# A conditional residual stack on one core: norm weights placed later, weight and output loads moved to the GpSimd queue, a third keys buffer and a fourth early product

## The chip, the cores and the metric

The program runs on one core of a Trainium2 chip. The time is the device time of one execution in microseconds (us). A core has a matrix engine (TensorE, PE in the rows; PEld is its weight load), VectorE (DVE), ScalarE (ACT), GpSimd (POOL) and SyncE (SP). SP issues most of the transfers, GpSimd issues the gathers. All data is float32.

## What is computed

`x` is 64 sequences of 32 rows by 512. Four layers follow one another, each added to its input:

```python
x = x + einsum('bct,bcd->bdt', x, L0_weights[condition])            # a 32x32 mix of the rows per sequence
x = x + x @ base.T + bias + (x @ A[adapter].T) @ B[adapter].T       # a linear layer with a low-rank part
# attention: 32 query heads, 8 key heads, D = 128, 512 cached keys by page table, 32 new ones
q, k, v = x @ Wq.T, x @ Wk.T, x @ Wv.T
q, k = rope(rmsnorm(q, q_norm_w), pos), rope(rmsnorm(k, k_norm_w), pos)
scores = where(valid, q @ concat(k_cache[table], k).T / sqrt(D), -1e30)
x = x + (softmax(scores) @ concat(v_cache[table], v)) @ Wo.T
x = x + einsum('bct,bcd->bdt', x, L3_weights[condition])            # the mix of rows again
```

## The kernel before

The 2048 rows are 16 tiles `t` of 128 rows, four sequences each. The key heads are in two groups `g` of four. A *step* is a tile of one group, 32 in all; a *unit* is one sequence of a step, 128 in all; a *slot* is one key head of a unit, 512 in all (n = 512). Slots before 0 hold the first layers, and after the last slot comes the output stage.

The order on each engine is written by hand. `at(slot, where, do, ...)` puts a piece of work into a plan, and `slot(i)` (L1120) emits the pieces of slot i in a fixed order: fetch, pool, then the scores of slot i, the transposes of slot i - 2, the projections (`pe`), powers, value products of slot i - 3, softmax division, VectorE work (`dve`), ScalarE work (`act`), stores (`store`). Each engine runs its own instructions in that order and waits where an operand is not there.

**First layers.** `First` (L380) makes one tile: the gather `mix_rows`, the block diagonal `mix_diag` of it on VectorE (L402), the matmul `mix_ps` (L411), the gathers `a_rows` and `b_rows`, transposes (L428), the low-rank product `h_ps` and the linear product `l_ps` with `base_sb` (L465). Beside them `angles()` (L296) loads the norm weights (`q_raw`, `k_raw`) and makes from them `q_cos`, `q_sin`, `k_cos`, `k_sin`, then the sines and cosines of all positions; it is a generator, taken on by `next(more)` between the slots (L1185 to L1190). In the prologue (L1153) the base weights (1 MB) and the bias are loaded ahead of it.

**Steps.** A pair of steps is projected together (`Plain` L559, `Block` L626) in the slots before it is used; the last projections are in slot 478. `Norm` scales and rotates the heads; its `rstd` (L683) is computed on GpSimd. `Unit` (L742) loads the 16 key pages of a sequence (`kT`, 64 KB each, L763) on SP into one of two buffers, at slot 4(u - 1); GpSimd gathers four blocks of values (`v_sb`, L105) in slots 4u - 1 to 4u + 2, into eight buffers. `store` (L897) writes the outputs `oT` of a step (1 MB) once in 16 slots.

**Weights.** They lie in spaces tagged w0 to w8, each reused: w6, w7 and w8 hold the angles first, then sums of query weights (`block_sum`). In the last pair of each group the next weights (`wv`, `wk`, `wq`, and at the end eight `wo`) are loaded in halves of 512 KB on SP, at fixed places after the pair's home slot (L1016).

**Output stage.** It multiplies 2 x 2 blocks with seven products instead of eight (L1281): a11, a12, a21, a22 are the outputs of two tiles and two groups (`o_in`, 1 MB each, loaded in halves by `fetch_o` while slots still run), s3 and two further sums are made of them (L1308 to L1312), and `third_weights` makes one weight combination. A product is 16 steps of 128x128 by 256 columns. Three of these products (`p1` of pairs 1, 2 and 0) are taken early, in slots 488 to 511 (`early_product`, L1090); pair 0's second product is the first of the output stage (L1317).

Of the kernel before, what the change touches and what calls it, by code (L numbers as in the profile page):

```python
# [27 lines left out]
F32 = mybir.dt.float32  # L28
# [23 lines left out]
NG = 2  # L52
# [25 lines left out]
def resid_kernel(  # L78
# [102 lines left out]
    def load_kv_weights(g, kind, i):  # L181

        if i == 0:
            w_sb[kind] = wpool.tile(
                [P, NC, KG * D], F32, name=f"w{'kv'[kind]}{g}", tag=f"w{kind}"
            )
        nc.sync.dma_start(
            out=w_sb[kind][:, :, i * 2 * D : (i + 1) * 2 * D],
            in_=wkv[2 * g + i][:, :, kind * 2 * D : (kind + 1) * 2 * D],
        )  # L190

    def load_q_weights(g, k, i):
        if i == 0:
            w_sb["q", k] = wpool.tile([P, NC, REP * D], F32, name=f"wq{g}_{k}", tag=f"w{2 + k}")
        part = slice(i * NC // 2, (i + 1) * NC // 2)
        nc.sync.dma_start(out=w_sb["q", k][:, part], in_=wq[KG * g + k][:, part])

    def load_o_weights(k, i):
        if i == 0:
            tag = f"w{(1, 0, 2, 3, 4, 5, 6, 7)[k]}"  # L200
            w_sb["o", k] = wpool.tile([P, REP, HID], F32, name=f"wo{k}", tag=tag)
        part = slice(i * REP // 2, (i + 1) * REP // 2)
        nc.sync.dma_start(out=w_sb["o", k][:, part], in_=wo[k][:, part])
# [21 lines left out]
    with ExitStack() as l2:  # L225
# [70 lines left out]
        def angles():  # L296
# [3 lines left out]
            for name, src, scale in (("q", q_norm, -SCALE * ROOT), ("k", k_norm, ROOT)):  # L300
                raw = start_pool.tile([P, 2, D // 2], F32, name=f"{name}_raw")
                nc.sync.dma_start(out=raw.rearrange("p a b -> p (a b)"), in_=across(src, D))
                for what in ("cos", "sin"):
                    norm_w[name, what] = start_pool.tile(
                        [P, 2, D // 2], F32, name=f"{name}_{what}"
                    )
                swapped = norm_w[name, "sin"]
                nc.vector.tensor_scalar(norm_w[name, "cos"], raw, scale, None, ALU.mult)
                nc.vector.tensor_scalar(swapped[:, 0, :], raw[:, 1, :], -scale, None, ALU.mult)
                nc.vector.tensor_scalar(swapped[:, 1, :], raw[:, 0, :], scale, None, ALU.mult)  # L310
            freq = start_pool.tile([P, D // 2], F32, name="freq")
            nc.sync.dma_start(out=freq, in_=across(inv_freq, D // 2))
            pos = start_pool.tile([P, NT], F32, name="pos")
# [11 lines left out]
            yield  # L325
# [33 lines left out]
            sine(0)  # L359

# [150 lines left out]
        last_scores = []  # L511

# [229 lines left out]
        class Unit:  # L742


            def __init__(self, u):
# [6 lines left out]
                self.kT = room["kT"].tile([P, NPP + 1, KG, PSIZE], F32, name="kT")  # L752
# [224 lines left out]
        for i in range(n_pairs):  # L977
# [31 lines left out]
            if p == NT // 2 - 1:  # L1009

                if g == NG - 1:
                    loads = [(load_o_weights, k) for k in range(2 * KG)]
                else:
                    loads = [(load_kv_weights, g + 1, k) for k in (1, 0)]
                    loads += [(load_q_weights, g + 1, k) for k in range(KG)]
                for w, load in zip((6, 11, 21, 23, 32, 34, 36, 38), loads):  # L1016
                    for j in (0, 1):
                        at(home + w + j, "store", *load, j)
# [37 lines left out]
        for c in range(NT):  # L1056

            home = -27 + c
            key = -1 - c
            at(home - 3 if c > 3 else begin + 2, "fetch", make, turn_of, key, Turn, 0, c, start_pool, (4, 2))  # L1060
            at(home, "turn", call, turn_of, key, "turn")
            at(home, "keep", call, turn_of, key, "keep")
            at(home + 1, "store", call, turn_of, key, "store")
            at(begin + 11 + c // 2, "dve", rotary, c)
            at(begin + 11 + c // 2, "store", store_rotary, c)
        for u in range(len(units)):
            at(KG * (u - 1) if u else ready, "fetch", make, unit_of, u, Unit, u)
# [11 lines left out]
        def fetch_o(name, g, t, i):  # L1079
            if i == 0:  # L1080
                early[name] = o_pools[0].tile([P, KG * REP, P], F32, name="o_in", tag=name)
            part = slice(i * KG * REP // 2, (i + 1) * KG * REP // 2)
            nc.sync.dma_start(out=early[name][:, part], in_=o_dram[g][t][:, part])
# [6 lines left out]
        def early_product(pair, name, i):  # L1090
            if i == 0:
                early["p1", pair] = ps_m.tile([P, HID], F32, name="proj_ps", tag="m")
            nc.tensor.matmul(  # L1093
                early["p1", pair][:, : HID // 2],
                lhsT=early[name][:, i, :],
                rhs=w_sb["o", i // REP][:, i % REP, : HID // 2],
# [4 lines left out]
        def early_keep(pair):  # L1101
            ps = early["p1", pair]
            early["p1", pair] = o_pools[0].tile([P, HID // 2], F32, name=f"p1_{pair}")
            nc.scalar.copy(early["p1", pair], ps[:, : HID // 2])  # L1104

        home = n - 24
        for j, (pair, name) in enumerate(((1, "a12"), (2, "a21"), (0, "a11"))):
            for i in (0, 1):
                at(home - 3 + 3 * j + i, "store", fetch_o, name, 0, 2 * pair, i)
            for i in range(KG * REP):  # L1110
                at(home + 8 * j + i // 2, "pe", early_product, pair, name, i)
            at(home + 8 * j + 7, "act", early_keep, pair)
        for i in (0, 1):
            at(home + 9 + i, "store", fetch_o, "a12", 1, 0, i)
            at(home + 12 + i, "store", fetch_o, "a22", 1, 1, i)
            at(home + 17 + i, "store", fetch_o, "a21", 0, 1, i)
# [36 lines left out]
        with tc.manual_schedule(engines=ENGINES):  # L1153
# [12 lines left out]
            slot(begin)  # L1166
            lora["base"] = first_pool.tile([P, NC, HID], F32, name="base_sb")
# [3 lines left out]

            lora["mask"] = []
            for i in (0, 1):

                mask_i = first_pool.tile([P, P], I32, name=f"mask_i{i}")
                nc.gpsimd.iota(
                    mask_i, pattern=[[-RANK, NB], [0, S]], base=-i * P // 2, channel_multiplier=1
                )
                low = small.tile([P, P], F32, name="mask_low", bufs=1)
                mask = first_pool.tile([P, P], F32, name=f"lora_mask{i}")  # L1180
                nc.vector.tensor_scalar(low, mask_i, 0.0, None, ALU.is_ge)
                nc.vector.tensor_scalar(mask, mask_i, float(RANK), None, ALU.is_lt)
                nc.vector.tensor_tensor(mask, mask, low, ALU.mult)
                lora["mask"].append(mask)
            more = angles()  # L1185
            next(more)
            for i in range(begin + 1, begin + 11):
                slot(i)
                for _ in range(2 if i < begin + 6 else 1):
                    next(more, None)  # L1190
# [43 lines left out]
    with ExitStack() as l3:  # L1234
# [46 lines left out]
        with tc.manual_schedule(engines=ENGINES):  # L1281
            waiting = []
            for pair in range(NT // 2):
# [33 lines left out]
                p_2 = product(a12, w21)  # L1317
# [110 lines left out]
```

## Time and profile before

| | us |
|---|---|
| median of 3 runs | 2552.29 (2546.11 to 2552.34) |
| the profiled execution | 2539.27 |
| its span | 2537.5 |

By stage, TensorE's busy time in windows of the span:

| window, us | what runs | PE busy, us | DVE busy, us | granted clock | GB/s |
|---|---|---|---|---|---|
| 0 to 63.4 | first layers begin | 42.76 | 36.56 | 1.00 | 276 |
| 63.4 to 126.8 | first layers | 59.51 | 40.53 | 1.00 | 275 |
| 126.8 to 200 | first layers end | 67.09 | 41.52 | 1.00 | 198 |
| 500 to 1000 | steps, group 0 | 499.65 | 365.20 | 1.00 | 195 |
| 1060 to 1085 | change of group | 22.58 | 17.48 | 1.00 | 255 |
| 1500 to 2000 | steps, group 1 | 499.32 | 368.33 | 1.00 | 186 |
| 2000 to 2050 | last projections, wo loads | 41.77 | 35.15 | 0.95 | 238 |
| 2050 to 2100 | last steps | 45.74 | 23.58 | 0.91 | 239 |
| 2100 to 2150 | last steps | 40.66 | 30.26 | 0.93 | 152 |
| 2200 to 2537.5 | output stage | 333.54 | 107.85 | 1.00 | 98 |

A row of the timeline has start, duration, engine (SPq is SP's queue of issues), line, operation, written and read tiles, form, count, and in brackets the idle time before it with what ended it. A busy TensorE is not one at its peak, since its matmuls are pipelined.

### The profile page before, as it was taken

The numbers are of one execution on the slowest core, as the hardware profiler recorded it, in microseconds if no ns is written. First come the engines' busy times: TensorE is split into PE (matmuls) and PEld (weight loads), VectorE is DVE, ScalarE is ACT, GpSimd is POOL, SyncE is SP. The second block draws the span as 40 slices with busy tenths as digits, with TensorE's granted clock in tenths as the row PEclk, the third lists the DMA queues.
The fourth block names the chain that finished last, engine by engine and source line by source line (L and its number), as shares of the span: only waits on it lengthen the run. The fifth ranks groups of instructions, "written<-read, shape, count | busy, mean of one in ns | idle before, by whom it ended". The sixth has DMA issues, their size and how long they took to land.

```text
span 2537.5 us, 46802 instructions
## 1 busy us (share of the span) xinstructions
PE 2473.9 (97%) x13824; PEld 1869.8 (74%) x13824; DVE 1665.4 (66%) x4150; ACT 1280.2 (50%) x3669; POOL 1072.5 (42%) x880
## 2 busy tenths in 40 slices
PE   6999999999999999999999999999999988999999
PEld 3556777777777777777777777777777777888887
DVE  5656767676767677777777677777776845533322
ACT  1336666666666666666666666666666643000000
POOL 4325555454545445454545545545554532000000
PEclk9999999999999999999999999999999989999999
DMA  8866666666667667766565556566666775333221
GB/s 276 275 193 200 189 192 187 190 194 186 200 189 205 177 199 215 255 185 201 165 192 169 181 174 186 168 183 180 182 177 210 210 254 168 126 105 127 103 84 59
DMA packets 444732, 463.60 MB, mean 183 GB/s; under 512 B 50624, under 2 KB 366912, under 8 KB 436672
## 3 DMA queue, kind: packets, MB, share of 16 engines
q1 hardware_dynamic: 401216, 321.64, 40.9%
q0 software_dynamic: 43264, 138.97, 18.5%
q8 instruction: 112, 1.84, 0.3%
q14 instruction: 140, 1.15, 0.1%
HBM read 389.12 MB, written 79.69 MB: 185 GB/s over the span
## 4 chain that ended last, share of the span: by engine, by line
PE 87%; DVE 3%; DMA 2%; ACT 1%; SPq 1%; issue 1%; ACTq 0%; DVEq 0%
PE o_ps L862 17%; PE out_ps L1256 14%; PE proj_ps L626 14%; PE s_ps L807 10%; PE proj_ps L559 8%; PE s_ps L810 8%; PE pT_ps L849 8%; PE head_ps L725 3%; PE o_ps L874 2%; DMA o<-oT 1%; PE l_ps L465 1%; DVE sm L815 1%; DVE rot_a L717 1%; PE proj_ps L1093 1%; PE mix_ps L1274 1%
## 5 line engine op out<-in xcount | busy, mean ns | idle before, releaser
L105 POOL DMA_INDIRECT v_sb<-v,v_rows x512 | 523.3, 1022 | 494.3 <-PE o_ps L862 397.3
L815 DVE CUSTOM_DVE_ANT_0 sm<-s_ps,pen 128x544 f32<-128x544 f32 x512 | 370.7, 724 | 472.2 <-PE s_ps L810 466.9
L862 PEld LDWEIGHTS o_ps<-pT,v_sb 128*128 128x128 f32 x4096 | 520.7, 192 | 137.3 <-issue 134.5
L826 ACT ACTIVATE sm<-sm,top 128x544 f32<-128x544 f32 x512 | 382.5, 747 | 472.2 <-DVE top L815 471.9
L862 PE MATMUL o_ps<-pT,v_sb 128*128 128x128 f32 x4096 | 542.3, 275 | 0.6 <-DMA v_sb<-v,v_rows 0.4
L832 ACT ACTIVATE sm<-sm,share 128x512 f32<-128x512 f32 x512 | 369.9, 723 | 185.8 <-DVE share L831 183.1
L683 POOL TENSOR_TENSOR rstd<-ss,minus_half 128x4 f32<-128x4 f32 x160 | 193.7, 1210 | 473.5 <-DVE ss L681 472.2
L807 PE MATMUL s_ps<-kT,qT 128*128 128x288 f32 x1024 | 347.4, 421 | 10.3 <-DMA kT<-kT 10.1
L851 DVE COPY pT<-pT_ps 128x512 f32<-128x512 f32 x512 | 351.2, 686 | 0.8 <-PE pT_ps L849 0.8
L849 PE MATMUL pT_ps<-ident,sm 128*128 128x128 f32 x2048 | 308.2, 273 | 1.9 <-ACT p L1104 1.7
L810 PE MATMUL s_ps<-kT,qT 128*128 128x256 f32 x1024 | 305.8, 380 | 2.7 <-DMA kT<-kT 2.6
L849 PEld LDWEIGHTS pT_ps<-ident,sm 128*128 128x128 f32 x2048 | 256.6, 141 | 54.0 <-ACT sm L832 1.8
L778 POOL TENSOR_SCALAR pen<-key_f,seq_f 128x544 f32<-128x544 f32 x128 | 280.3, 2190 | 12.2 <-DMA xS<-x 1.6
L810 PEld LDWEIGHTS s_ps<-kT,qT 128*128 128x128 f32 x1024 | 194.7, 190 | 57.5 <-DMA kT<-kT 4.2
L676 ACT ACTIVATE sq<-raw 128x128 f32<-128x128 f32 x640 | 189.8, 298 | 33.6 <-DVE raw L638 29.7
L105 POOL DMA_INDIRECT mix_rows<-in_w,cond_rows x32 | 32.7, 1022 | 347.7 <-DVE mix_diag L168 301.0
L807 PEld LDWEIGHTS s_ps<-kT,qT 128*128 128x128 f32 x1024 | 155.0, 191 | 27.7 <-issue 10.9
L1307 ACT COPY p<-out_ps 128x256 f32<-128x256 f32 x5 | 1.9, 373 | 333.8 <-PE out_ps L1256 333.8
L1256 PE MATMUL out_ps<-w,o_in 128*128 128x256 f32 x768 | 167.1, 379 | 0.0
L833 DVE TENSOR_SCALAR p_new<-sm,share 128x32 f32<-128x32 f32 x512 | 148.6, 290 | 18.2
L1256 PEld LDWEIGHTS out_ps<-w,o_in 128*128 128x128 f32 x768 | 145.9, 190 | 19.8
L638 DVE TENSOR_TENSOR raw<-proj_ps,raw 128x512 f32<-128x512 f32 x224 | 150.4, 683 | 14.2 <-PE proj_ps L626 14.2
(149 smaller groups left out, 3422.4 us busy)
## 6 DMA issues: line engine op xcount, KB each, us to landing
kT<-kT SPq DMA_DIRECT2D x2048, 64.0 KB
o<-oT SPq DMA_DIRECT2D x32, 1024.0 KB
o_in<-o SPq DMA_DIRECT2D x28, 1024.0 KB
rot<-rot SPq DMA_DIRECT2D x48, 256.0 KB
page_rows<-in_kv_cache SPq DMA_DIRECT2D x32, 256.0 KB
wq<-in_wq SPq DMA_DIRECT2D x16, 512.0 KB
vn<-v_rows SPq DMA_DIRECT2D x32, 256.0 KB
v<-in_kv_cache SPq DMA_DIRECT2D x32, 256.0 KB
```

The lines of the kernel that those rows point to most:

```text
L105: nc.gpsimd.indirect_dma_start(out=dst, out_offset=None, in_=table, in_offset=bass.IndirectOffsetOnAxis(ap=index, axis=0),)
L626: nc.tensor.matmul(self.ps, lhsT=self.pair.x[x][:, half][:, c, :], rhs=blocks(self.b)[w][:, c, :], start=(c == 0), stop=(c == 1),)
L778: nc.gpsimd.tensor_scalar(self.pen, key_f, seq_f[:, self.b : self.b + 1], BIG, ALU.is_ge, ALU.mult)
L807: nc.tensor.matmul(ps[:, first:HID], lhsT=q, rhs=self.kT[:, :n1, k, :], start=True, stop=True)
L810: nc.tensor.matmul(ps[:, HID : first + LA], lhsT=q, rhs=self.kT[:, n1:, k, :], start=True, stop=True)
L815: nc.vector.tensor_tensor_reduce(out=sm, in0=ps[:, first : first + LA], in1=self.pen, scale=1.0, scalar=3e38, op0=ALU.add, op1=ALU.min, ac ...
L826: nc.scalar.activation(sm, sm, AF.Exp, bias=top, scale=-1.0, accum_out=total)
L832: nc.scalar.activation(sm[:, :L], sm[:, :L], AF.Copy, scale=share)
L849: nc.tensor.transpose(ps[:, c, :], self.sm[k][:, c * P : (c + 1) * P], ident)
L851: nc.vector.tensor_copy(pT, ps)
L862: nc.tensor.matmul(self.o_ps[k], lhsT=self.v[c][:, k * D : (k + 1) * D], rhs=self.pT[k][:, c, :], start=(c == 0), stop=False,)
L1256: nc.tensor.matmul(ps[:, :HALF], lhsT=o[:, i, :], rhs=w[i // REP][:, i % REP, :], start=(i == 0), stop=(i == KG * REP - 1),)
```

## The change

1. `angles()` issues its three small loads ahead of base and bias, and makes the norm weights last, behind the second sine. The two masks (now `own_ranks(i)`) are made in slot begin + 2, after the first diagonals; the other pieces of the angles are taken two a slot from begin + 3 on.
2. The loads of the second group's weights and of `wo`, and all of `fetch_o`, are issued by GpSimd. The last `wo` comes four slots later.
3. Units 122 and 125 put their keys into the space w8, and the keys of units 122 to 127 are fetched eight slots ahead of use.
4. Four products are taken early: `p1` of pairs 1, 2, 0 from slots 479, 488, 496, and pair 0's second product (`p2`) over slots 504 to 514. The first takes its outputs from the space w7.

```diff
-    def load_kv_weights(g, kind, i):
+    def load_kv_weights(g, kind, i, queue=nc.sync):
...
-        nc.sync.dma_start(
+        queue.dma_start(
...
-            for name, src, scale in (("q", q_norm, -SCALE * ROOT), ("k", k_norm, ROOT)):
-                raw = start_pool.tile([P, 2, D // 2], F32, name=f"{name}_raw")
-                nc.sync.dma_start(out=raw.rearrange("p a b -> p (a b)"), in_=across(src, D))
...
+            raw_of = {}
+            for name, src in (("q", q_norm), ("k", k_norm)):
+                raw_of[name] = start_pool.tile([P, 2, D // 2], F32, name=f"{name}_raw")
+                nc.sync.dma_start(
+                    out=raw_of[name].rearrange("p a b -> p (a b)"), in_=across(src, D)
+                )
             freq = start_pool.tile([P, D // 2], F32, name="freq")
             nc.sync.dma_start(out=freq, in_=across(inv_freq, D // 2))
+            yield
...
             sine(0)
+            yield
+            for name, scale in (("q", -SCALE * ROOT), ("k", ROOT)):
+                raw = raw_of[name]
...
+                nc.vector.tensor_scalar(norm_w[name, "cos"], raw, scale, None, ALU.mult)
+                nc.vector.tensor_scalar(swapped[:, 0, :], raw[:, 1, :], -scale, None, ALU.mult)
+                nc.vector.tensor_scalar(swapped[:, 1, :], raw[:, 0, :], scale, None, ALU.mult)
...
+        def own_ranks(i):
+            mask_i = first_pool.tile([P, P], I32, name=f"mask_i{i}")
+            nc.gpsimd.iota(
+                mask_i, pattern=[[-RANK, NB], [0, S]], base=-i * P // 2, channel_multiplier=1
+            )
...
+            nc.vector.tensor_tensor(mask, mask, low, ALU.mult)
+            return mask
...
-                self.kT = room["kT"].tile([P, NPP + 1, KG, PSIZE], F32, name="kT")
+                pool, tag = (wpool, "w8") if self.u in spare else (room["kT"], "kT")
+                self.kT = pool.tile([P, NPP + 1, KG, PSIZE], F32, name="kT", tag=tag)
...
-                for w, load in zip((6, 11, 21, 23, 32, 34, 36, 38), loads):
+                places = [6, 11, 21, 23, 32, 34, 36, 38]
+                if g == NG - 1:
+                    places[-1] += 4
+                for w, load in zip(places, loads):
                     for j in (0, 1):
-                        at(home + w + j, "store", *load, j)
+                        at(home + w + j, "store", *load, j, nc.gpsimd)
...
+        spare = range(len(units) - 6, len(units), 3)
         for u in range(len(units)):
-            at(KG * (u - 1) if u else ready, "fetch", make, unit_of, u, Unit, u)
+            early_by = u >= spare[0]
+            at(KG * (u - 1 - early_by) if u else ready, "fetch", make, unit_of, u, Unit, u)
...
             if i == 0:
-                early[name] = o_pools[0].tile([P, KG * REP, P], F32, name="o_in", tag=name)
+                pool, tag = (o_pools[0], name) if name else (wpool, "w7")
+                early[name] = pool.tile([P, KG * REP, P], F32, name="o_in", tag=tag)
             part = slice(i * KG * REP // 2, (i + 1) * KG * REP // 2)
-            nc.sync.dma_start(out=early[name][:, part], in_=o_dram[g][t][:, part])
+            nc.gpsimd.dma_start(out=early[name][:, part], in_=o_dram[g][t][:, part])
...
+        home = n - 33
+        for key, name, g, fetches, begins, over in (
+            (("p1", 1), None, 0, -5, 0, 8),
+            (("p1", 2), "a21", 0, 6, 9, 8),
+            (("p1", 0), "a11", 0, 9, 17, 8),
+            (("p2", 0), "a12", 1, 13, 25, 11),
+        ):
+            for i in (0, 1):
+                at(home + fetches + i, "store", fetch_o, name, g, 2 * key[1], i)
+            for i in range(KG * REP):
+                at(home + begins + i * over // (KG * REP), "pe", early_product, key, name, i)
+            at(home + begins + over - 1, "act", early_keep, key)
+        for i in (0, 1):
+            at(home + 18 + i, "store", fetch_o, "a22", 1, 1, i)
+            at(home + 20 + i, "store", fetch_o, "a21", 0, 1, i)
         home = n - 24
-        for j, (pair, name) in enumerate(((1, "a12"), (2, "a21"), (0, "a11"))):
...
             slot(begin)
+            more = angles()
+            next(more)
             lora["base"] = first_pool.tile([P, NC, HID], F32, name="base_sb")
...
             for i in range(begin + 1, begin + 11):
                 slot(i)
-                for _ in range(2 if i < begin + 6 else 1):
+                if i == begin + 2:
+                    lora["mask"] = [own_ranks(0), own_ranks(1)]
+                for _ in range(2 if i > begin + 2 else 0):
                     next(more, None)
...
-                p_2 = product(a12, w21)
+                p_2 = early.get(("p2", pair))
+                if p_2 is None:
+                    p_2 = product(a12, w21)
```

## The prediction

> **What bounds the kernel now.** I read the page's engine shares first, then TensorE's waits, the windows around those waits, the chain and the SP queue there. The page:
>
> ```profile
> PE 2473.9 (97%) x13824; PEld 1869.8 (74%) x13824; DVE 1665.4 (66%) x4150; ACT 1280.2 (50%) x3669; POOL 1072.5 (42%) x880
> ```
>
> The span is 2537.5 us, so TensorE idles for 63.6 us: that, and matmuls run at a lowered clock, is all a change without fewer matmuls can win. Its waits (us, times, longest):
>
> ```profile
> PE mix_ps L411 <- DVE mix_diag L402: 19.3, 2, 18.3
> PE s_ps L807 <- DMA kT<-kT: 10.1, 3, 4.8
> ...
> PE proj_ps L1093 <- DMA o_in<-o: 4.3, 1, 4.3
> ```
>
> One wait of 18.3 us is the start, the others are the last steps. The start, in the timeline (start, us, instruction, idle before it):
>
> ```profile
> 14.39 0.23 DVE L308 TENSOR_SCALAR q_cos<-q_raw 128x128 f32<-128x128 f32 x1 [3.75 <-DMA q_raw<-in_q_norm]
> ...
> 17.98 0.28 DVE L402 TENSOR_TENSOR mix_diag<-mix_rows,same 128x128 f32<-128x128 f32 x1
> 18.32 0.50 PEld L411 LDWEIGHTS mix_ps<-x_sb,mix_diag 128*128 128x128 f32 x2 [18.32 <-DVE mix_diag L402]
> ```
>
> VectorE takes the first diagonal only after the norm weights, and these wait for a load that stands behind 1 MB of base weights on SP. The last steps, by windows of 10 us (length, busy us of PE, PEld, DVE, ACT, POOL, clock, DMA share, GB/s):
>
> ```profile
> 2030.00:2040.00 10.00, 8.82 (x71) 7.80 (x69) 8.04 (x21) 6.48 (x14) 4.65 (x4) 1.00 1.00 379
> 2040.00:2050.00 10.00, 4.92 (x28) 3.31 (x21) 2.39 (x7) 3.16 (x8) 5.34 (x5) 0.77 0.89 240
> 2050.00:2060.00 10.00, 5.74 (x23) 4.58 (x22) 1.83 (x5) 1.56 (x3) 0.00 (x0) 0.55 0.86 280
> ...
> 2110.00:2120.00 10.00, 5.59 (x19) 4.52 (x20) 1.83 (x5) 1.56 (x3) 3.15 (x3) 0.68 0.79 245
> ```
>
> TensorE is starved twice, and its granted clock falls with it. What SP issued before the first of the two:
>
> ```profile
> 2025.79 1.45 SPq L203 DMA_DIRECT2D wo<-in_wo  x3
> ...
> 2029.84 0.33 SPq L897 DMA_DIRECT2D o<-oT  x1
> 2030.96 15.65 SPq L763 DMA_DIRECT2D kT<-kT  x16
> 2046.66 0.90 SPq L203 DMA_DIRECT2D wo<-in_wo  x2
> 2047.67 0.36 SPq L1083 DMA_DIRECT2D o_in<-o  x1
> ```
>
> Sixteen key loads need 15.65 us to issue where 9.37 us do with nothing large ahead (at 2003.11). As built, each queue's DMAs share eight completion counters in turn, so an issue waits for the transfer eight before it. SP's waits from 1990 us on agree: L763 waited 6.2 us for wo, 5.8 for o_in, 4.8 for o<-oT. The same happens once in mid-kernel: 2.4 us at 1078 us, behind wq and a store of o.
>
> **The change, part by part**, against the profiled execution (2539.27 us, of which 2537.5 is the span).
>
> *Start.* The six norm-weight operations (1.2 us) move behind the angles, the masks behind the first diagonal, the three small loads ahead of base and bias. The first diagonal now waits for its gather alone: issued at 5.04; gathers of this form land in 2.2 to 7.4 us, so at 7.2 to 12.4; by their median in the first 60 us, 5.2, I take 10. The transpose of a_rows is next in TensorE's order; that gather, issued at 6.46, lands by its median of 7.0 at about 13. Before, it started at 20.18. So the chain starts about 7 us sooner. The base weights are issued some 2 us later but are first used 4 us after the transpose. Is 7 us kept? From 40 to 200 us TensorE idles only 10 us and the DMA share is 0.6 in 40 to 50 us, so transfers catch up. VectorE is the risk: 9.6 of 10 us busy in 20 to 30 us; the same work now has less room. I take **-6.5**; ends -9 and -2.
>
> *Keys.* Units 122 and 125 use the w8 space, free after slot 478, and from 122 on keys are fetched eight slots ahead, not four. The stalls stand at slots 488 and 504, where units 122 and 126 begin; both loads followed an o store. Stall one: 5.08 + 4.26 = 9.3 us idle, plus slow matmuls (L807 took 1.30 us for 0.65, L810 1.22 for 0.59, and so on to the o_ps group 1.79 for 1.06): 3.5 us. Stall two: 1.1 + 4.4 = 5.5 idle plus 2.8 slow. Together **-21.1** if all is gone. Late next is unit 121, still fetched four slots ahead, beside wo.
>
> *Early products.* No matmul is added: one product more goes into the slots, and one leaves the end. A slot there is (chain: start, us, what):
>
> ```profile
> 2061.57 0.89 PE o_ps L862 x8
> 2062.47 0.49 PE s_ps L807 x2
> 2062.95 0.43 PE s_ps L810 x2
> 2063.38 0.44 PE pT_ps L849 x4
> ```
>
> 2.25 us, with 0.54 more in four slots, so 2.4; a product's share adds 0.87, eight times 6.95 us. Slots 479 to 487 ran from 2014.55 to about 2042.5, 28 us for nine slots of 2.4 (plus four head transposes of 0.44): VectorE set their pace. The p1 product put there uses idle TensorE time; in 2010 to 2040 that is 3.15 us, of which I take **-2.5**. Slots 504 to 514 get the 16 steps of a product over eleven slots. Their VectorE load is no smaller but earlier: s3 and the two sums of the outputs (3 x 2.29) move from slots 508 to 511 to 503 and 504, where 1.9 us of VectorE work a slot leaves 1.35; so some 4 us of stall move there, in place of the 3.8 us idle in 2130 to 2150. **-0.5**. They wait for a21, issued three slots (10 us) ahead; the half load of o_in at 2047.67 took 7.9 us to land.
>
> *Loads through GpSimd.* Forty loads of 512 KB leave SP: 12 at the change of head group, 16 of wo, 12 of o. SP's keys then wait for keys and o stores only; in mid-kernel **-2** of that 2.4. On GpSimd each costs about what a gather does: L105, 1.02 us. The Trainium skill, "SBUF — State Buffer", the 'DVE blocks DMA' trap, speaks against this: DMAs issued from GpSimd need it to write descriptors, VectorE's two-port copies lock it out, and one of 620 ns took 3100. Row: in 20 to 30 us, with VectorE 9.6 busy, gathers took at most 1.76. By the rule each load adds some 3 us to GpSimd, by the row 1.0 to 1.8. Behind it in order stand the value gathers and rstd. The tightest gather seen, issued at 2012.59, was needed at 2017.9 and stalled TensorE 0.36 us; landing is 3.8 in the median, so 1.5 us is spare. The fourth gather of a unit is the critical one. In mid-kernel three loads stand right ahead of one (slots 197, 213, 225), two more one gather further (212, 224). In the last steps there is no rstd, and the fourth gather goes out 10.5 us before use (2071.08 for 2081.6). By the row: 3 x (1.0 issue + 1.5 for 512 KB at 350 GB/s - 1.5 spare) = **+3**. By the rule 3 us of issue in place of 1.0: 9, and 15 with the two others. I take the row, which is of this kernel. Below nothing it cannot go. The loads' own waits for space cost nothing: wo7 waits for the p1 product in its space, over three slots before, a21 for the product that ends at slot 495, four before; the gathers behind them would be the ones delayed.
>
> *Bandwidth.* The Trainium skill's "DMA: Bandwidth & Descriptors", section Issuing engines are not separate DMA queues, says that all queues end on the same 16 engines, so another issuer only saves issue time. By that, bytes set the tail: about 10.6 MB passed from 2016 to 2055.6, 268 GB/s, where eight slots of 3.25 give 26 us; at an unchanged rate stall one stays, worth 12.8. The row of 2030 to 2040 shows 379 GB/s, so 28 us: 2 us short. Stall windows of 240 and 280 say that issue, not the engines, held it back. I take the row with 1 us for unit 121: **+3**.
>
> Sum: -6.5 - 21.1 - 2.5 - 0.5 - 2 + 3 + 3 = -26.6. The profiled time 2539.3 becomes 2512.7. The median shown, 2552.29, lies 13.0 above that execution; I carry this offset: **2525.7**, say 2526.
>
> **The rivals.**
> 1. *Bytes bind.* The tail stays at about 270 GB/s, stall one returns (+12.8 less the 3 counted). For it: shares of 0.86 to 0.89 within the stall, and 10 MB of loads, 2 MB of keys and values a unit, in slots 474 to 503. Against: 379 GB/s just before. 2526 + 10 = 2536; with the start's worst end as well 2540.
> 2. *Gathers starve* (slower). Values queue behind 512 KB loads on GpSimd's one queue. If a load holds a gather by the 7.9 us that o_in took, each of the five in mid-kernel stalls 7.9 + 1.0 - 1.5 = 7.4, and the lowered clock adds 3.5/9.3 of that, as in stall one: 10.2 each, 51 in all. 2526 - 3 + 51 = 2574. It decides from (26.6 + 3) / 5 = 5.9 us a load, clock included; below that the change still gains. For it: one gather already came late. Against: a lone load waits behind no other large one here.
> 3. *The start gives nothing*: VectorE or loads take back all 6.5: 2532. For it: VectorE at 9.6; against: the load it waited for goes.
> 4. *All is absorbed*: no stall at 121 or 503, start at -9: 2526 - 6 - 4 - 2.5 = 2513.
>
> **How the numbers follow.** Forecast 0.58, rival 1 0.22, rival 2 0.08, rival 3 0.06, rival 4 0.06. The range 2512 to 2545 takes in all but rival 2 and outer tails. 0.3%, about what a measurement can tell, is 7.7 us: faster is below 2544.6. Forecast, 3 and 4 give 0.69 of that, rival 1 0.17: 0.86. Rival 1's far end leaves 0.05 and rival 2's mild form 0.01 within: 0.06. Slower 0.08.
>
> **What would show it.** First mix near 10 us, first aT transpose near 13; no wait of L807 or its successor for kT at slots 488 and 504, clock 1.00 through the last steps except at slot 503; SP's sixteen key issues back near 9 to 10 us; GpSimd loads near 1 us each, and TensorE's waits for v_sb below 5 us in all. Rival 1 shows as kT or o_in waits at DMA shares near 1.0; rival 2 as o_ps waits for v_sb after a wv, wk or wq load. I am wrong if the wait moves to s3 (VectorE on a21), or if the start merely waits for other loads by 200 us.

## The result, and the profile after

| | before | after |
|---|---|---|
| median of 6 runs | 2552.17 (2546.11 to 2552.81) | 2533.80 (2529.47 to 2537.50) |
| the profiled execution | 2539.27 | 2537.50 |
| its span | 2537.5 | 2535.7 |

The ratio is 0.9932, 95% interval [0.9919, 0.9945]: 18.4 us less between the medians. The forecast was 2526, 7.8 us too low and inside its range. The two profiled executions differ by only 1.8 us, so the first question is how far they can be compared; the experiments begin there.

TensorE's waits in the kernel after (us, times, longest):

```profile
PE mix_ps L417 <- DVE mix_diag L408: 15.0, 1, 15.0
PE o_ps L883 <- ACT oT L912: 7.6, 1, 7.6
...
PE out_ps L1278 <- DVE o_in L1342: 3.2, 1, 3.2
PE proj_ps L1122 <- ACT p L1133: 3.1, 2, 2.6
...
PE o_ps L883 <- DMA kT<-kT: 1.9, 1, 1.9
```

The waits of the scores for keys, 12.7 us before, are gone, and so is the 4.3 us for `o_in`. New is a wait of 7.6 us of the value product for `oT`, the outputs of a step, which ScalarE copies out of PSUM. The start waits 15.0 us instead of 18.3, where 10 were foreseen. The last row is a value product of the last projections, at 1993 us; at the same place after_again, a second execution of this kernel, names `v_sb`. What SP issued ahead of the new wait, from the timeline of its queue (start, duration):

```profile
2022.28 25.42 SPq L784 DMA_DIRECT2D kT<-kT  x32
2047.75 0.57 SPq L806 DMA_DIRECT2D v_new<-vn  x1
2048.43 0.38 SPq L918 DMA_DIRECT2D o<-oT  x1
2049.63 17.76 SPq L784 DMA_DIRECT2D kT<-kT  x16
```

And ScalarE, in the timeline of the same kernel:

```profile
2049.22 0.36 ACT L1133 COPY p<-proj_ps 128x256 f32<-128x256 f32 x1
2057.61 0.27 ACT L909 COPY oT<-o_ps 128x128 f32<-128x128 f32 x1 [8.02 <-DMA o<-oT]
```

Units 121 and 122 are both fetched at slot 480, one four slots ahead and one eight. Their 32 key loads stand in one row on SP's queue, and behind them the store of the third-last step's `oT`, due at slot 483. `oT` has a single buffer: ScalarE may not write the next step's outputs until that store has landed, 9.2 us after it was issued. TensorE waits for ScalarE, and its clock falls, as the windows show (length, busy us of PE, PEld, DVE, ACT, POOL, clock, DMA share, GB/s):

```profile
2040.00:2050.00 10.00, 10.00 (x71) 8.86 (x70) 6.30 (x18) 5.77 (x13) 4.91 (x6) 1.00 0.87 283
2050.00:2060.00 10.00, 2.40 (x14) 2.09 (x13) 1.83 (x5) 2.10 (x5) 7.06 (x8) 0.77 1.01 378
2060.00:2070.00 10.00, 10.00 (x58) 8.66 (x58) 4.82 (x13) 3.89 (x8) 0.00 (x0) 0.89 0.66 228
```

The keys arrive in time now, but a store has taken their place as the thing that comes late. The start, in VectorE's timeline of the kernel after:

```profile
4.69 0.17 DVE L151 TENSOR_SCALAR lora_rows<-lora_rows_f 128x8 int32<-128x8 f32 x1
14.69 0.29 DVE L408 TENSOR_TENSOR mix_diag<-mix_rows,same 128x128 f32<-128x128 f32 x1 [9.83 <-DMA mix_rows<-in_w,cond_rows]
```

As foreseen, the first diagonal waits for its gather alone. But that gather, issued at 5.02, takes 9.7 us until VectorE starts, not the 5 of the forecast.

### The profile page after: what moved, and what is told of

Read it like the earlier page. It is cut to its first block, busy times and chain, and to the rows that moved or that the text cites. A ratio compares the mean times of both kernels' runs of the same rounds, so it can differ in the third digit from the quotient of the medians.

```text
span 2535.7 us, 46802 instructions
## 1 busy us (share of the span) xinstructions
PE 2479.9 (98%) x13824; PEld 1873.1 (74%) x13824; DVE 1664.8 (66%) x4150; ACT 1279.8 (50%) x3670; POOL 1096.5 (43%) x920
## 4 chain that ended last, share of the span: by engine, by line
PE 89%; DMA 2%; DVE 2%; ACT 1%; issue 1%; POOL 0%; SPq 0%; DVEq 0%; ACTq 0%
PE o_ps L883 17%; PE proj_ps L646 15%; PE out_ps L1278 14%; PE s_ps L828 10%; PE pT_ps L870 8%; PE s_ps L831 8%; PE proj_ps L579 8%; PE head_ps L745 3%; PE o_ps L895 2%; PE l_ps L471 1%; DMA kT<-kT 1%; PE proj_ps L1122 1%; DMA v_sb<-v,v_rows 1%; PE s_ps L863 1%; PE mix_ps L1296 1%
## 5 line engine op out<-in xcount | busy, mean ns | idle before, releaser
L799 POOL TENSOR_SCALAR pen<-key_f,seq_f 128x544 f32<-128x544 f32 x128 | 281.0, 2196 | 12.7 <-DMA xS<-x 1.4
```

The costliest lines, as they stand in the source:

```text
L799: nc.gpsimd.tensor_scalar(self.pen, key_f, seq_f[:, self.b : self.b + 1], BIG, ALU.is_ge, ALU.mult)
```

## The experiments

### Are the two executions comparable?

The kernels before and after were each run once more.

> The kernel before, profiled a second time. The first profiled execution took 2539.3 us, some 13 us less than the median of the other executions (2552.2), while that of the kernel after (2537.5) stands 4 us above its median. Theory A: the execution shown was lucky, and a second one, near 2550 us, has the missing time as longer idles of TensorE at the waits for keys (slots 488 and 504, about 2040 to 2125 us). Theory B (a rival): the missing time is spread over the whole kernel as short waits or slower matmuls, so the windows up to 2010 us are longer by most of 10 us and those behind it are as they were. Theory C: it is again near 2539 us and the two offsets differ by what lies outside the span.

Measured: 2537.88, on a chip where 43 runs of before have the median 2541.0. None of the theories saw the cause: the time depends on the chip, or on the occasion, since each chip was used on one. Before has medians of 2541.0, 2550.0 and 2540.3 us on the three chips of the experiments, and had 2552.2 in the first comparison. Its profiled execution of 2539.3 fits the two quick chips, so the 13.0 us that the forecast carried as an offset are most likely a distance between chips.

> The kernel after once more, beside before on the same chip. Chips differ: before had a median of 2541 us on one and 2550 us on another, so the ratio is what is read. Theory A (the change is worth the same on every chip): 0.993, 16 to 19 us less than before. Theory B (on a chip on which before takes 2541 us, and so is near its profiled execution of 2539 us, the gain is smaller, since that part of it which the profiled executions don't show, 1.8 against 18 us, comes with the slower chip): 0.996 to 0.998 there, 0.993 on a slower one.

Measured: 2524.78 (2522.33 to 2526.68) where before takes 2540.29 on the same chip, a ratio of 0.9932 [0.9918, 0.9945], once more. Theory A holds, with 15.5 us by these medians just under its 16: the ratio is the same on a quick chip and on a slow one. The first profile of after is one of the six executions of the first comparison, so of a slower chip, and this second one, with a span of 2523.4, is the one to set beside before's.

Where an execution gains or loses can be read from landmarks. A good one is the store of a step's outputs, which SP issues once in each step. Its time against the profiled before (270.8, 1060.9, 1126.0, 1972.0, and the span's end 2537.5), in us:

| kernel | step 0 | step 13 | step 14 | step 28 | end |
|---|---|---|---|---|---|
| before_again | +0.6 | +1.3 | +0.7 | +0.6 | -1.4 |
| after (slower chip) | +0.2 | +2.7 | +1.5 | +2.8 | -1.8 |
| after_again | -2.8 | -2.8 | -4.6 | -4.8 | -14.1 |
| start_only | -1.8 | -0.5 | -0.9 | -0.9 | -0.1 |
| keys_only | +2.4 | +3.5 | +3.0 | +3.0 | +7.9 |
| queues_only | -0.8 | 0.0 | -1.9 | -2.0 | -1.8 |
| keys_queues | -0.2 | -0.2 | -2.1 | -2.2 | -2.8 |
| products_only (slower chip) | +1.8 | +5.5 | +6.4 | +8.3 | +10.4 |
| after_sp (slower chip) | -2.1 | +2.2 | +3.7 | +5.1 | +8.6 |
| after_store (slower chip) | -3.4 | -1.9 | -3.7 | -1.5 | -11.1 |
| after_small_later (slower chip) | +4.3 | +7.9 | +6.0 | +7.4 | -1.5 |
| after_store_again | -3.8 | -2.5 | -4.4 | -4.6 | -19.9 |
| after_four | -1.9 | -1.7 | -3.6 | -3.8 | -24.2 |

On the quick chips hardly anything moves between steps 0 and 28, 1700 us of the same work, but for the change of group around steps 13 and 14. On the slower ones the lag grows by 1.9 to 7.2 us there, in slips of about 0.7 to 1 us. Some of these show among TensorE's waits, as one line of the kernel after on the slower chip:

```profile
PE proj_ps L579 <- ACT raw L596: 2.6, 5, 0.7
```

and the same line of after_again, on a quick one:

```profile
PE proj_ps L579 <- ACT raw L596: 0.7, 1, 0.7
```

Why ScalarE's copy is late there was not tried. Before was not profiled on a slower chip, but products_only, which is the same kernel up to step 28, loses 6.5 us between steps 0 and 28 there. For what follows, times are compared by ratio, and traces from step 28 to the end.

### One part at a time

Each kernel is before with one of the four parts.

```diff
 # start_only: item 1 of the change alone
 # keys_only: item 3 alone
...
+        spare = range(len(units) - 6, len(units), 3)
...
+            early_by = u >= spare[0]
+            at(KG * (u - 1 - early_by) if u else ready, "fetch", make, unit_of, u, Unit, u)
 # queues_only: item 2 alone, with the last wo in its old place
 # products_only: item 4 alone, inputs loaded by nc.sync, the last wo four slots later
```

> Before with the start alone changed (norm weights, masks and angles reordered). Theory A: the first mix comes some 3 us earlier, the gather and not VectorE now ends its wait, and the end moves by as much: 2547 to 2549 us (3 to 5 us less than before). Theory B (the whole 18 us of the gain came from the start, since keys only changed places with the store): about 2538 us. Theory C (the start gives nothing, other loads take over by 200 us): 2552 us.

Measured: 2538.64, 2.4 us less than before, ratio 0.999 [0.9982, 0.9998]. Theory A's mechanism, with an effect slightly below its numbers. In the seven executions that have the new start as it stands, VectorE took the first diagonal at 12.8 to 14.7 us, against 17.3 to 18.4 in the six with the old one, and the landmark of step 0 lies at -2.2 in their mean, against +0.6 in the six with the old start.

> Before with the third keys buffer and the earlier fetch of the last six units alone. Theory A: the two waits for keys (12.8 and 8.3 us with the slow matmuls behind them) go, but 32 key loads in one piece stand ahead of the store of oT on SyncE's queue, so that TensorE waits 7 to 8 us for oT near 2050 us and works slowly behind it, about 10 us in all; net 9 to 13 us less: 2539 to 2543 us. Theory B (a pure exchange of waits): within 3 us of before, 2549 to 2555 us. Theory C (the store's wait is caused by the other loads of the change): the full 21 us, about 2531 us, and no wait for oT.

Measured: 2546.05, ratio 1.0017 [1.0010, 1.0023]: **5 us slower than before**. All three theories were wrong. A and C forecast a gain, and B nothing beyond 3 us. A named the wait for `oT`, but neither its length nor the wait for `o_in`. TensorE's waits:

```profile
PE o_ps L863 <- ACT oT L892: 11.5, 1, 11.5
PE proj_ps L1097 <- DMA o_in<-o: 9.2, 1, 9.2
```

and SP's queue in the same kernel:

```profile
2019.40 20.15 SPq L764 DMA_DIRECT2D kT<-kT  x32
2039.60 1.43 SPq L203 DMA_DIRECT2D wo<-in_wo  x3
...
2042.39 1.38 SPq L898 DMA_DIRECT2D o<-oT  x1
2044.59 17.29 SPq L764 DMA_DIRECT2D kT<-kT  x16
...
2062.94 0.36 SPq L1087 DMA_DIRECT2D o_in<-o  x1
```

Two things stand behind key loads here: the store, and the loads of `o_in` for an early product, which come 16 keys later still. The two waits, 20.7 us, are longer than what TensorE waited for keys and `o_in` before, 17.0 us, and of the waits for keys 3.0 us stay.

> Before with the loads of the output weights and of the sums' inputs issued by GpSimd instead of SyncE, all else as it was. Theory A: TensorE is not held by these loads on either queue; the gathers behind them cost it a wait of some 2 us once, the keys come as late as before: 2550 to 2555 us. Theory B (GpSimd's queue starves the gathers): 2560 us or more. Theory C (SyncE's queue, freed of 10 to 18 loads near slots 470 to 500, issues keys sooner): 2544 to 2548 us, with shorter waits for kT near 2045 and 2115 us.

Measured: 2540.44, ratio 0.9996 [0.9987, 1.0004], no difference. Theory A. The waits changed hands within it. TensorE waits 5.8 us for `v_sb`, in four pieces, and the scores of slot 488 wait longer than before:

```profile
PE s_ps L807 <- DMA v_new<-vn: 9.4, 1, 9.4
```

SP's queue ahead of it, and the window of the wait:

```profile
2027.72 0.34 SPq L897 DMA_DIRECT2D o<-oT  x1
2028.85 19.71 SPq L763 DMA_DIRECT2D kT<-kT  x16
```

```profile
2040.00:2050.00 10.00, 2.53 (x15) 1.71 (x13) 1.74 (x5) 2.51 (x7) 6.75 (x7) 0.72 1.06 383
```

The row of the waits names the load of the new values, which uses a completion counter that keys use too. The scores read keys, and these were all issued only at 2048.56. With the other loads gone from SP's queue the scores begin at 2054.29, where before they began at 2047.89. So GpSimd's queue alone did not bring the keys forward. A store still stands ahead of them, and the DMA share was 1.06; which of the two held them was not separated.

> Before with four early output products (instead of three) in the last 33 slots alone, their inputs loaded by SyncE. Theory A: 32 more matmuls of 0.65 us move from behind the loop to in front of its end, where TensorE has idle time only in the waits for keys; what is filled there is at most 2 to 5 us, the rest is moved and not removed: 2547 to 2551 us. Theory B: the product moved ahead fills the waits for keys nearly whole: 2540 us or less. Theory C: the inputs loaded by SyncE ahead of keys make these later: 2553 to 2558 us.

Measured: 2547.60 where before takes 2550.04, ratio 0.9991 [0.9983, 0.9999]. Theory A: about 2.4 us.

Added up, the four parts are worth -2.4 + 5.0 - 0.6 - 2.4 = -0.4 us. Together they are worth some -16 on a quick chip. Nearly all of the gain is in how they meet.

### Which of them meet

```diff
 # keys_queues: items 2 and 3 together (old start, three early products)
 # after_sp: the kernel after, loads back on SP
...
-                        at(home + w + j, "store", *load, j, nc.gpsimd)
+                        at(home + w + j, "store", *load, j)
...
-            nc.gpsimd.dma_start(out=early[name][:, part], in_=o_dram[g][t][:, part])
+            nc.sync.dma_start(out=early[name][:, part], in_=o_dram[g][t][:, part])
```

> Before with the third keys buffer and early fetch, and with the output weights and the sums' inputs loaded by GpSimd, but with the old start and the three old early products. Keys alone made the kernel 5 us slower (TensorE waited 11.5 us for oT and 9.2 us for an o_in that stood behind key loads on SyncE's queue), queues alone gave 0.6 us. Theory A (the two only pay together: GpSimd's queue takes the o_in and wo loads out of the keys' way, the wait for o_in goes, the one for oT stays at 7 to 8 us): 8 to 12 us less than before, ratio 0.995 to 0.997. Theory B (the product placed ahead is needed too, to fill what is left of the waits): 0.998 to 1.001. Theory C (no interaction, the sum of both): 1.001 to 1.002.

Measured: 2537.14, ratio 0.9986 [0.9976, 0.9997], 3.2 us less than before: theory B. The wait for `o_in` is gone, so GpSimd's queue did what theory A said of it, but the one for `oT` has not shrunk, and the sums of the outputs now hold up the scores through VectorE:

```profile
PE o_ps L863 <- ACT oT L892: 11.7, 1, 11.7
PE s_ps L808 <- DVE top L816: 5.4, 1, 5.4
```

In after_again, which adds the start and the four early products, the same two groups are

```profile
PE o_ps L883 <- ACT oT L912: 5.7, 1, 5.7
...
PE s_ps L828 <- DVE top L836: 0.4, 1, 0.4
```

6.0 us less for `oT`. That is close to a product's 6.95 us, the forecast's figure, and the product that begins at slot 479 lies ahead of this wait. The store itself is no earlier: counted from the store of step 28 it is issued after 71.7 us here and 72.1 us there. Thus TensorE reaches the wait later, with a product done. Items 2, 3 and 4 without the start were not run, so this reading is an inference from the two traces. From step 28 to the end the two kernels gain 0.6 and 9.3 us.

> The kernel after with its loads of output weights and sums' inputs back on SyncE's queue. Theory A: the wait for oT near 2050 us grows, since these loads share SyncE's queue with 32 key loads and the store: 2 to 6 us slower than after, 2536 to 2540 us, while the gathers' wait near 1995 us (1.9 us) goes. Theory B (the queue makes no difference): 2534 us. Theory C (the gathers behind GpSimd's loads cost more than the queue of SyncE): 2530 us or less.

Measured: 2545.57 where before takes 2550.04, ratio 0.9984 [0.9973, 0.9995]. By the ratios (0.9932 for after) the GpSimd queue is worth some 13 us inside the whole change, and 0.6 alone. That rests on two chips. Theory A had the direction and a third of the size: with the loads on SP, TensorE waits 8.2 us for `oT` and 6.4 us for `o_in`.

### The store out of the keys' way

```diff
 # after_store
-                nc.sync.dma_start(out=o_dram[self.g][self.t], in_=oT_of.pop(self.s))
+                queue = nc.scalar if self.s == len(steps) - 3 else nc.sync
+                queue.dma_start(out=o_dram[self.g][self.t], in_=oT_of.pop(self.s))
```

> The kernel after with one DMA moved: the store of oT of the third-last step is issued by ScalarE instead of SyncE, and so stands behind no key loads. Theory A (the store behind 32 key loads is what TensorE waited 7.6 us for): the wait for oT near 2050 us goes with the slow matmuls behind it, 8 to 10 us: 2524 to 2526 us, near the forecast of 2526. Theory B (the wait is for bandwidth; the store lands late wherever it is issued, or another wait takes its place): 2531 to 2534 us.

Measured: 2527.20 where before takes 2550.04, ratio 0.9908 [0.9892, 0.9925]. The wait for `oT` is gone from its trace. By the ratios it takes some 6 us less than after, between the two theories. Since after itself was not run on this chip, the kernel was repeated beside after.

> The kernel after with the one store of oT issued by ScalarE, now beside after on one chip. Theory A (the store behind 32 key loads cost what TensorE waited, with the slow matmuls behind): 5 to 10 us less than after, ratio to before 0.989 to 0.991. Theory B (a wait for bytes takes its place: in the first run of this kernel the queues moved 343 to 363 GB/s from 2030 to 2050 us and TensorE idled 3.9 us at 2040 to 2050): 0 to 4 us less than after.

Measured: 2519.53 (2518.55 to 2524.61) against 2524.78 for after, ratio to before 0.9919 [0.9904, 0.9933]: 5.3 us less than after, theory A at its lower end (its ratio just beyond it). One DMA on another queue did it. What writes or reads `oT` from 2020 to 2050 us in after_store_again (line, engine, count, ns, first and last start):

```profile
L909 ACT COPY oT<-o_ps x2: 257/262/267, 2024.8 to 2038.9; 128x128 f32<-128x128 f32 x2
...
L919 ACTq DMA_DIRECT2D o<-oT x1: 345/345/345, 2028.1 to 2028.1; - x1
```

The store goes out at 2028.1 instead of 2038.88, and ScalarE copies the next step's outputs at 2038.9 instead of 2047.97, with no wait. Some of TensorE's wait stays, as theory B said. The windows of after_store_again:

```profile
2030.00:2040.00 10.00, 10.00 (x73) 8.84 (x72) 5.99 (x19) 6.32 (x15) 4.91 (x6) 1.00 1.01 375
2040.00:2050.00 10.00, 8.16 (x41) 6.73 (x40) 4.07 (x13) 3.12 (x6) 6.47 (x8) 0.83 1.04 347
2050.00:2060.00 10.00, 10.00 (x71) 8.78 (x70) 5.14 (x14) 5.61 (x13) 5.08 (x5) 1.00 0.81 258
```

TensorE still idles 1.8 us from 2040 to 2050, at a DMA share above 1, and its clock dips once. The wait is for keys, most of it in one piece:

```profile
PE s_ps L828 <- DMA kT<-kT: 1.5, 1, 1.5
```

The last kernel of this group moves the last two stores as well and changes three more things, each against one of the waits left.

```diff
 # after_four
+                queue = nc.scalar if self.s >= len(steps) - 3 else nc.sync
...
-                    places[-1] += 4
+                    places[4:] = [34, 38, 42, 46]
...
-            (("p1", 2), "a21", 0, 6, 9, 8),
-            (("p1", 0), "a11", 0, 9, 17, 8),
+            (("p1", 2), "a21", 0, 6, 9, 7),
+            (("p1", 0), "a11", 0, 9, 17, 7),
...
+                p_2 = early.get(("p2", pair))
+                if p_2 is not None:
+                    nc.vector.tensor_tensor(a12, a12, a11, ALU.subtract)
                 add(x3[0][:, lo], x3[0][:, lo], p1)
...
```

> The kernel after with four changes to its last steps: the last three stores of oT issued by ScalarE; the difference a12 - a11 of the first pair made ahead of the additions to x3 (3.2 us of TensorE's wait); two early products issued in 7 slots instead of 8, so that their PSUM bank is copied out before the next one begins (2.6 us of wait); and the second group's output weights loaded over slots 481 to 494 instead of 479 to 490, apart from the 32 key loads. Theory A (these four waits are what TensorE still loses there, and nothing takes their place): 12 to 18 us less than after, ratio to before 0.986 to 0.989. Theory B (keys and weights are bound by bytes until slot 494, so that the wait moves to keys or values): 5 to 9 us less than after, 0.990 to 0.991.

Measured: 2515.40 (2514.99 to 2516.04), ratio to before 0.9898 [0.9883, 0.9913]: 24.9 us less than before and 9.4 less than after. It lies between the two theories. The bytes fit once the weights are spread:

```profile
2030.00:2040.00 10.00, 10.00 (x69) 9.02 (x68) 7.16 (x19) 5.74 (x12) 5.13 (x7) 1.00 0.93 309
2040.00:2050.00 10.00, 10.00 (x72) 8.84 (x71) 5.63 (x17) 6.25 (x15) 8.47 (x9) 1.00 1.01 351
2050.00:2060.00 10.00, 9.88 (x66) 8.49 (x65) 4.85 (x13) 4.71 (x11) 6.50 (x7) 1.00 1.05 361
2060.00:2070.00 10.00, 10.00 (x73) 8.89 (x73) 5.30 (x16) 5.88 (x15) 4.61 (x6) 1.00 0.99 317
```

TensorE is busy almost without a break at a clock of 1.00, with the DMA share at 0.99 to 1.05 for 30 us on end. What is left in the last steps waits for VectorE, at 2090 to 2130:

```profile
PE s_ps L828 <- DVE top L836: 2.7, 1, 2.7
PE s_ps L863 <- DVE top L836: 2.7, 2, 2.3
```

How the 9.4 us divide among the four edits was not separated, but for the store's 5.3.

### The small loads of the start

```diff
 # after_small_later: base and bias first; the three small loads two slots later
-            more = angles()
-            next(more)
             lora["base"] = first_pool.tile([P, NC, HID], F32, name="base_sb")
...
+            more = angles()
...
                     lora["mask"] = [own_ranks(0), own_ranks(1)]
+                    next(more)
```

> The kernel after with the three small loads that spread one row over all partitions (two norm weights, the frequencies) issued behind the base weights, the bias and two slots of work instead of ahead of them. Theory A (these loads hold up the first gather, which took 9.6 us from issue to landing): the gather lands in 5 to 6 us, the first mix comes at 10 to 11 us instead of 15.0, and the end moves 2 to 4 us: 2530 to 2532 us. Theory B (the gather waits for the loads of x or for its own start, as any first gather): first mix at 15 us, 2534 us. Theory C: the first mix is early, but the work waits for base weights or others before 200 us, and the end stands at 2534 us.

Measured: 2539.20 where before takes 2550.04, ratio 0.9959 [0.9946, 0.9971]: some 7 us slower than after by the ratios, which none of the theories saw. The landmark of step 0 has it already, at +4.3 against -2.2. The gather came no later than elsewhere, but the frequencies came too late, for work that stands ahead of the second diagonal on VectorE:

```profile
DVE angles L321 <- DMA freq<-in_inv_freq: 8.4, 1, 8.4
DVE mix_diag L408 <- DMA mix_rows<-in_w,cond_rows: 7.9, 1, 7.9
```

From its issue at 5.20 the gather still took 7.7 us until VectorE used it, against 7.7 to 9.7 in the seven executions with the small loads ahead. These explain 2 us at most, and why the first gather is slow is not explained.

## Why the prediction was right or wrong, point by point

**The total** was right within its range, and in part by the width of that range. The sum of -26.6 was too large by 12.5 us against the profiled executions on quick chips (-14.1 for after_again) and by 8.2 us between the medians first shown. By the landmarks some 11 us are missing in the last steps and some 4 at the start. The measured 2533.8 lies nearer to the numbers of rival 3 (2532) and rival 1 (2536) than to 2526, and came about as neither of them says. The offset of 13.0 could be carried, since the ratio is the same on quick and slower chips.

**Keys, -21.1: the step that failed.** Right: no scores wait for keys at slots 488 and 504 in after or after_again, and "Late next is unit 121" looked at the right place. Wrong was what it took to be late there. The step on GpSimd's loads read SP's queue in one direction, "SP's keys then wait for keys and o stores only", and neither of the two steps asked what waits behind keys. Two units' loads at one slot hold a store that is due three slots later and whose buffer is single. By itself this part costs 5 us; with GpSimd's queue it gains 3.2 for the two (0.6 from step 28 on); with the products as well 9.3 from step 28 on. Only with the store elsewhere does that stretch come to -15.3, and with after_four's edits to -20.4. The forecast's terms for that stretch (-21.1 - 2.5 - 0.5 + 3, and some of the gathers' +3) come to about -20: it priced a kernel with the store and some smaller waits out of the way. Nor did sixteen key loads go back to 9 or 10 us of issue: behind the store they took 17.76 us in after and 18.74 in after_again, and the sixteen after the 32 took 11.05 in after_store_again, where ScalarE issues the store.

**Early products, -2.5 and -0.5**, were too small in this company. They were priced as filler for 3 us of idle time; beside the others, the wait for `oT` that follows the first of them is 6.0 us shorter, by the inference above. Alone they are worth the 2.4 measured, near the forecast. One cost was overlooked: with pair 0's `p2` taken early, nothing is left to multiply while VectorE makes a12 - a11 (L1342), and TensorE waits for it at the start of the output stage, 3.0 to 3.3 us in each trace that has the early `p2` but after_four's, where the difference is made sooner.

**Start, -6.5.** The mechanism was right and the size wrong: a gain of 2.4 in the runs. The mis-sized term is the landing of the first gather, taken as 5 us from the median of similar ones, measured at 7.7 to 9.7 until VectorE uses it. In the means, the transpose of a_rows comes 4.1 us sooner (16.0 for 20.1), not 7, and 2.8 us of it are left at step 0. The low end of that step, -2, was the better number.

**Change of group, -2.** From step 13 to 14 the five kernels on quick chips with the loads on GpSimd gain 1.8 to 1.9 us on the profiled before, and the three with the loads on SP 0.4 to 0.6. Of the 2 us some 1.4 are the queue's. Right, and slightly large.

**Gathers behind GpSimd's loads, +3.** TensorE waits 3.0 us for `v_sb` in after_again: 1.1 us at 1015 us, where three such stalls were forecast, and 1.9 at 1985, in the last projections, where none was. In queues_only it waits 5.8, above the 5 foreseen, and the kernel still comes out at -0.6. The size was right, the places in part. A 512 KB load costs GpSimd 0.56 to 0.86 us in after_again, less than the 1.02 assumed. The 'DVE blocks DMA' trap of the Trainium skill's "SBUF — State Buffer", weighed at 3 us a load, is not seen in these durations.

**Bandwidth, +3.** The queues could carry 347 to 375 GB/s, as the row of before said, and a wait of some 2 us stays at 2040 to 2050 once the store is moved. Right, though the bytes were counted low: the profile of before has 280 GB/s from 2016 to 2055.6, not 268, and these bytes at 379 are 3 us short instead of 2. The statement of the Trainium skill's "DMA: Bandwidth & Descriptors" (section Issuing engines are not separate DMA queues) that another issuer only saves issue time fits queues_only, 0.6 us at a DMA share of 1.06. It does not tell what the order on a queue is worth: some 13 us inside the change, by ratios from two chips.

**The rivals.** Bytes did not bind at 270 GB/s. Near 350 GB/s and above they may have in part: rival 1's sign, keys late at DMA shares near 1.0, stands in queues_only at full length, with a store ahead of the keys as well, and in after_store_again, without that store, with 1.8 us. Gathers did not starve; the start gave more than nothing. The clock did not stay at 1.00: 0.77 behind the store in after, 0.81 in after_again.

## What to carry to other kernels

When a load is issued earlier, list what is issued behind it on its queue and when each is due, stores as well: a store that frees a single buffer is a deadline like any load's. Parts of a change can be worth nothing one by one and much together, so take parts out of the whole as well as adding one to the old kernel. And compare two traces only after a landmark in work that the change doesn't touch has shown that they run alike.

## What the runs showed of the hardware

The same kernel took 2540.3 to 2552.2 us in the median from one chip or occasion to another, while the ratio of the two kernels was 0.9932 both at 2552.2 and at 2540.3.

A wait can cost more than its length. Behind the 5.7 us for `oT`, in after_again's timeline of TensorE:

```profile
2040.90 0.50 PE L895 MATMUL o_ps<-pT_new,v_new 32*128 32x128 f32 x8
2041.33 0.75 PE L828 MATMUL s_ps<-kT,qT 128*128 128x288 f32 x2
2041.92 0.59 PE L831 MATMUL s_ps<-kT,qT 128*128 128x256 f32 x2
...
2048.67 2.08 PE L883 MATMUL o_ps<-pT,v_sb 128*128 128x128 f32 x8 [5.71 <-ACT oT L912]
2050.54 1.17 PE L828 MATMUL s_ps<-kT,qT 128*128 128x288 f32 x2
2051.50 1.06 PE L831 MATMUL s_ps<-kT,qT 128*128 128x256 f32 x2
```

Two score groups take 1.17 and 1.06 us where they took 0.75 and 0.59 ahead of the wait, and eight value matmuls take 2.08 us, where a group of eight took 1.05 at 2039.92. That is 1.9 us more in these three groups. The granted clock in after_again was 1.00 from 2030 to 2040, 0.85 from 2040 to 2050 and 0.81 from 2050 to 2060.

A 1 MB store issued while key loads follow it took 9.1 us to free its buffer in after_again (issued at 2038.88, ScalarE's copy at 2047.97), at a DMA share of 0.96.
